# Four weight loads issued by GpSimd instead of SP in a cross-attention and FFN kernel

## The chip, the cores and the metric

The kernel runs on one core of a Trainium2 chip. The core has five engines that follow their own instruction queues: TensorE (PE in the profile: matmuls and transposes), VectorE (DVE), ScalarE (ACT), GpSimd (POOL) and SyncE (SP), which here does nothing but issue DMA transfers. Sixteen DMA engines move the data between HBM and the on-chip memory SBUF. The metric is the device time of one execution in microseconds; lower is better. Before the change it is 720.79 us, the median of 3 runs (720.69 to 720.82).

## The reference

A cross-attention block and a quantized feed-forward block, each on a layer-normed input and each with a residual. x is 8 batches of 112 tokens of width 512; the context is 8 batches of 375 rows of width 256; there are 16 heads of width 128, and the hidden width of the feed-forward block is 2048.

```
x = x + xattn(layernorm(x), ctx, Wq, Wk, Wv, Wo, gq, gk)
x = x + ffn(layernorm(x), W1, B1, W2, B2)

xattn: q = rmsnorm(h @ Wq) * gq;  k = rmsnorm(ctx @ Wk) * gk;  v = ctx @ Wv   (per head)
       out = softmax(q k^T / sqrt(128)) v;  return out @ Wo
ffn:   rows of X and all of W are rounded to int8 steps by their largest absolute value
       gelu(Xq @ W1q^T * scales + B1), quantized again, @ W2q^T * scales + B2
```

Wq is 512 x 2048, Wk and Wv are 256 x 2048, Wo is 2048 x 512, all in float32.

## The kernel before

**Tiling.** The heads are taken in groups of four (NG = 4 groups, 512 columns each), the batches in pairs (NPAIR = 4 pairs). A step on a pair and a group is numbered G = 0 to 15, a step on a batch and a group u = 0 to 31. The weights do not stay on chip: for each G the kernel loads again the column group of Wq (1 MB), Wk (0.5 MB) and Wv (0.5 MB), and the row group of Wo (1 MB). Every row that a load moves is 2 KB long in HBM.

**Work of one G.** Queries (line 532) and keys (650) are made by TensorE; VectorE and ScalarE norm them. Keys, queries and probabilities have to be transposed. Most of that goes by way of HBM: VectorE transposes blocks of 32 x 32, SP sends the blocks to a scratch buffer in HBM (keys: line 707, tile kd; probabilities: 807, pd; queries: 587, qd), and SP fetches them back in the new order (keys: 714, tile kT; probabilities: 817, pT; queries: 619, qr). Then come scores (758), the softmax (771 to 791), the weighted context (860, which reads pT), values (887, which read wv) and the projection (910, which reads wo).

**The quantized weights of the feed-forward block** are made in the first 200 us from eight pieces of 1 MB that SP loads at line 307: VectorE finds the largest value of each piece (line 315) and of all (321), GpSimd takes the largest over the partitions (322), and VectorE scales (328) and rounds.

**Order.** All steps have short names, and four long scripts (line 1214 on) give the order in which the whole kernel is written down: for instance `lq.3` is load_wq(3), `lk`, `lv` and `lo` are the other three loads, `Q0` and `Q1` the queries, `k0` to `k2` the keys, `kf` and `pf` the fetches of kT and pT. In later scripts the numbers are relative to the pair. The function in_written_order (line 77) ties each instruction to the one before it on the same engine, for the engines in this list:

```
ORDERED = (ENG.PE, ENG.DVE, ENG.Activation, ENG.SP)          # line 26
```

GpSimd is not in the list; there the framework (Tile) places instructions by its own rule, and each engine then executes its queue in order. Semaphore waits are put in by Tile for all engines.

**The queue before.** SP issues every transfer. GpSimd issues none: it clears small constants and the four probability buffers at the start (line 111), and does two all-reduces over partitions (line 322, steps ja.0 and ja.1).

**Buffers of the weights.** The tags in wpool decide what a load waits for. wq and wo have one buffer each, wv one, wk two. wq_1 sits in wo's buffer (line 211), wv_15 in one of wk's (226), wo_15 in wq's (232). So a load waits until the last matmul that reads the tile before it in the tag is done: load_wq(G) for the queries of G - 1 (wq_2 for those of G = 0), load_wk(G) for the keys of G - 2, load_wv(G) for the values and load_wo(G) for the projection of G - 1. wq_0, wq_1, wk_1 and wv_0 go to buffers that nothing has used. wk_0 is loaded in two halves with the first context by load_half (line 220), beside the function that the change edits for the others.

**The start.** The first script begins

```
cz.0 lk.0 cz.1 lf.0 lf.1 lx.0 l7.0 gl.0 lc.1 kh.0 jl.0 lk.1 lq.0 jl.3 jl.6 kh.1 xs.1 xs.0 ...
```

lf.0 and lf.1 load the halves of wk_0 and of the first context, lx.0 the first two batches of x, l7.0 the last batch of x, gl.0 the gains, lc.1 the second context (tile cT_1), jl.n the pieces of the feed-forward weights; kh, xs and what follows is work on other engines.

Of the kernel before, what the change touches and what calls it, by code (L numbers as in the profile page):

```python
# [30 lines left out]
def xattn_ffn_kernel(  # L31
# [16 lines left out]
    nc = tc.nc  # L48
    P = 128
# [7 lines left out]
    NG = INNER // (HG * D)  # L57
    GW = HG * D
# [65 lines left out]
    n = 1  # L124
# [84 lines left out]

    def load_wq(G):  # L210
        t = wpool.tile([P, KC, GW], F32, tag="wo" if G == 1 else "wq", name=f"wq_{G}")
        nc.sync.dma_start(out=t, in_=wq[:, bass.ts(G % NG, GW)].rearrange("(k p) n -> p k n", p=P))
        T["wq", G] = t

    def load_wk(G):
        t = T["wk", G] = wpool.tile([P, KCC, GW], F32, tag="wk", name=f"wk_{G}", bufs=2)
        if G > 0:
            nc.sync.dma_start(out=t, in_=wk[:, bass.ts(G % NG, GW)].rearrange("(k p) n -> p k n", p=P))

    def load_half(k):  # L220

# [3 lines left out]
    def load_wv(G):  # L225
        tag, bufs = ("wk", 2) if G == NGG - 1 else ("wv", 1)
        t = wpool.tile([P, KCC, GW], F32, tag=tag, name=f"wv_{G}", bufs=bufs)
        nc.sync.dma_start(out=t, in_=wv[:, bass.ts(G % NG, GW)].rearrange("(k p) n -> p k n", p=P))
        T["wv", G] = t

    def load_wo(G):
        t = wpool.tile([P, HG, C], F32, tag="wq" if G == NGG - 1 else "wo", name=f"wo_{G}")
        nc.sync.dma_start(out=t, in_=wo[bass.ts(G % NG, GW), :].rearrange("(h p) c -> p h c", p=P))
        T["wo", G] = t

    def pad_context(b):
# [26 lines left out]
    def load_biases(_):  # L263
        after(("jr", 2 * NP - 1))
        nc.sync.dma_start(out=b1_sb, in_=b1.partition_broadcast(P))
        nc.sync.dma_start(out=b2_sb, in_=b2.partition_broadcast(P))

    step("lq", NG, load_wq)
    step("lk", NG, load_wk)
    step("lv", NG, load_wv)  # L270
    step("lo", NG, load_wo)
    step("cz", BP, pad_context)
    step("lc", BP, load_context)
# [1128 lines left out]
```

## Time and profile before

| what | value |
|---|---|
| median of 3 runs | 720.79 us (720.69 to 720.82) |
| the profiled execution: its own time | 720.28 us |
| its span, first to last instruction | 718.5 us |
| TensorE clock granted | 0.999 of full speed |
| DMA: all on SP's queue, q1 | 131200 packets, 187.32 MB, 85.1% of 16 engines' span |
| DMA: two queues that fetch instructions | 46 packets, 0.53 MB |
| HBM read, written | 124.55 MB, 59.45 MB |

The profile shows one execution. Busy time is the time in which an engine ran an instruction; the busy time of TensorE's matmuls (PE) and of its weight loads (PEld) overlap. A row "A <- B: 4.7, 3, 2.8" in a table of waits says that A stood idle for 4.7 us in total, 3 times, at most 2.8 us, until B was done. A row of DMA issues gives the tile written, the tensor read, the queue, how many, KB of each and the median time from issue to landing, which is when the data is there. A row of a timeline gives start, duration, engine, line and operation, and in brackets the idle time before it and what ended it.

### The profile page before, as it was taken

The page shows a single profiled execution, that of the slowest core. Times are in us where ns is not written, and L with a number is a line of the kernel's source. Part 1 is how long each engine was busy: PE and PEld are TensorE (multiplying, and loading weights), DVE is VectorE, ACT ScalarE, POOL GpSimd, SP SyncE. Part 2 cuts the span into 40 slices and gives each one's busy share as a digit, 9 for nine tenths or more (in the row PEclk, how much of TensorE's full clock was granted, in tenths as well). Part 3 has the DMA queues.
Part 4 walks back from the last instruction along what each step waited for, and adds up shares of the span by engine and source line. Part 5 has one row for each costly group of instructions (what it writes and reads, how often), then busy time and mean ns, then how long its engine had stood idle before and what let it go on. Part 6 is the DMA issues. An engine that isn't in the chain of part 4 may idle for free.

```text
span 718.5 us, 8555 instructions
## 1 busy us (share of the span) xinstructions
PE 702.7 (98%) x2398; PEld 413.3 (58%) x2410; DVE 537.3 (75%) x1234; ACT 433.6 (60%) x1129; POOL 2.4 (0%) x10
## 2 busy tenths in 40 slices
PE   9999999999999999999999999999999999999976
PEld 4444456655657564745656465564657455667742
DVE  6997888887876677747857787868774898964395
ACT  5677576636475756556466556666755566627325
POOL 0000000000000000000000000000000000000000
PEclk9999999999999999999999999999999999999999
DMA  8799999989988999999898989999999889998201
GB/s 304 266 280 298 294 298 282 301 268 290 282 308 244 293 285 313 269 275 310 227 289 286 295 265 287 287 240 305 292 257 291 237 256 272 259 290 282 34 1 44
DMA packets 131246, 187.85 MB, mean 261 GB/s; under 512 B 34864, under 2 KB 90800, under 8 KB 130560
## 3 DMA queue, kind: packets, MB, share of 16 engines
q1 hardware_dynamic: 131200, 187.32, 85.1%
q8 instruction: 19, 0.31, 0.2%
q14 instruction: 27, 0.22, 0.1%
HBM read 124.55 MB, written 59.45 MB: 256 GB/s over the span
## 4 chain that ended last, share of the span: by engine, by line
PE 85%; DVE 5%; ACT 4%; DMA 3%; SPq 1%; issue 1%; POOL 0%; ACTq 0%; DVEq 0%; POOLq 0%
PE pkk L650 19%; PE pu L860 17%; PE pw L910 13%; PE pq L532 12%; PE sc L758 10%; PE po L887 6%; PE py L1159 2%; PE ph L1080 2%; DMA pT<-pd 1%; PE pkk L660 1%; DMA kT<-kd 1%; ACT probs L780 1%; DMA qr<-q 1%; DMA qss<-s 1%; ACT qsq L547 1%
## 5 line engine op out<-in xcount | busy, mean ns | idle before, releaser
L650 PE MATMUL pkk<-wk,cT 128*128 128x512 f32 x372 | 171.8, 593 | 0.3 <-DVE hid L1089 0.3
L860 PE MATMUL pu<-pT,c 128*128 128x448 f32 (+1 forms) x384 | 152.3, 540 | 1.0 <-DMA pT<-pd 1.0
L860 PEld LDWEIGHTS pu<-pT,c 128*128 128x128 f32 (+1 forms) x384 | 72.5, 190 | 71.3 <-issue 61.7
L780 ACT ACTIVATE probs<-sc,bias,rq 112x375 f32<-112x375 f32 x128 | 84.1, 663 | 47.8 <-DVE bias L773 47.8
L650 PEld LDWEIGHTS pkk<-wk,cT 128*128 128x128 f32 x372 | 70.0, 190 | 72.3 <-issue 60.9
L910 PEld LDWEIGHTS pw<-oT,wo 128*128 128x128 f32 x544 | 98.2, 190 | 9.8 <-issue 6.5
L910 PE MATMUL pw<-oT,wo 128*128 128x224 f32 (+1 forms) x544 | 101.8, 343 | 0.6 <-ACT oT L897 0.6
L532 PE MATMUL pq<-wq,xnT 128*128 128x512 f32 x224 | 100.2, 592 | 0.0
L758 PE MATMUL sc<-kT,qT 128*112 128x384 f32 x256 | 92.4, 486 | 0.3 <-DMA kT<-kd 0.2
L670 ACT COPY kk<-pkk 128x512 f32<-128x512 f32 x96 | 55.2, 580 | 58.6 <-DVE kz L698 25.6
L797 DVE STREAM_TRANSPOSE pz<-probs 128x384 f32<-128x384 f32 x120 | 63.7, 558 | 21.1 <-ACT probs L791 18.2
L791 ACT ACTIVATE probs<-probs,inv 112x375 f32<-112x375 f32 x128 | 72.1, 605 | 8.9 <-DVE inv L788 8.9
L771 DVE TENSOR_REDUCE top<-sc 112x1 f32<-112x375 f32 x128 | 63.8, 535 | 18.0 <-PE sc L758 17.5
L681 DVE TENSOR_REDUCE kss<-ksq 128x4 f32<-128x512 f32 x96 | 63.1, 668 | 14.0 <-ACT ksq L675 14.0
L532 PEld LDWEIGHTS pq<-wq,xnT 128*128 128x128 f32 x224 | 42.4, 190 | 49.6 <-issue 46.5
L758 PEld LDWEIGHTS sc<-kT,qT 128*112 128x112 f32 x256 | 44.7, 177 | 38.9 <-issue 16.7
L675 ACT ACTIVATE ksq<-kk 128x512 f32<-128x512 f32 x96 | 59.5, 628 | 6.4 <-DVE kss L681 6.0
L688 DVE TENSOR_TENSOR kk<-kk,rk 128x512 f32<-128x512 f32 x96 | 62.9, 675 | 0.5
L698 DVE STREAM_TRANSPOSE kz<-kk 128x512 f32<-128x512 f32 x93 | 62.3, 690 | 0.9 <-issue 0.4
L871 ACT COPY wc<-pu 128x448 f32<-128x448 f32 x64 | 33.5, 531 | 36.6 <-PE pu L860 36.6
L887 PEld LDWEIGHTS po<-wc,wv 128*128 128x128 f32 x272 | 49.1, 190 | 8.0 <-issue 4.1
L887 PE MATMUL po<-wc,wv 128*128 128x224 f32 (+1 forms) x272 | 53.1, 344 | 0.0
(122 smaller groups left out, 590.8 us busy)
## 6 DMA issues: line engine op xcount, KB each, us to landing
kd<-kz SPq DMA_DIRECT2D x124, 192.0 KB, 4.0
kT<-kd SPq DMA_DIRECT2D x31, 768.0 KB, 6.4
pT<-pd SPq DMA_DIRECT2D x30, 672.0 KB, 6.1
pd<-pz SPq DMA_DIRECT2D x90, 192.0 KB, 4.4
wq<-in_wq SPq DMA_DIRECT2D x16, 1024.0 KB, 7.7
wo<-in_wo SPq DMA_DIRECT2D x16, 1024.0 KB, 7.8
wv<-in_wv SPq DMA_DIRECT2D x16, 512.0 KB, 5.8
wk<-in_wk SPq DMA_DIRECT2D x15, 512.0 KB, 6.2
```

Source lines behind the costliest of these rows:

```text
L532: nc.tensor.matmul(pq[:, :GW], T["xnT", p][:, k, i * P : (i + 1) * P], T["wq", G][:, k, :], start=(k == 0), stop=(k == KC - 1),)
L650: nc.tensor.matmul(pk[:, :GW], T["cT", batch_of(u)][:, k, j * P : (j + 1) * P], T["wk", u // BP][:, k, :], start=(k == 0), stop=(k == KCC ...
L681: nc.vector.tensor_reduce(T["kss", u][:, j, :], T.pop(("ksq", u, j)).rearrange("p (h d) -> p h d", d=D), AX.X, ALU.add)
L688: nc.vector.tensor_tensor(kv, kv, T["rk", u][:, j, :].unsqueeze(2).to_broadcast([P, HG, D]), ALU.mult)
L758: nc.tensor.matmul(sc[:S, :SKP].rearrange("p (j i r) -> p j i r", j=NJ, r=BK), T["qT", G, i][:, h, :], T["kT", u][:, :, :, h, :].rearrange ...
L771: nc.vector.tensor_reduce(top[:, h : h + 1], T["sc", u, h0 + h][:S, :SK], AX.X, ALU.max, negate=True)
L780: nc.scalar.activation(p_bufs[h][:S, :SK], T["sc", u, h][:S, :SK], AF.Exp, bias=T["bias", u, h0][:, h - h0 : h - h0 + 1], scale=rq_of(u, h ...
L791: nc.scalar.mul(p_bufs[h][:S, :SK], p_bufs[h][:S, :SK], T["inv", u][:, h : h + 1])
L797: nc.vector.transpose(T["pz", u][:, :, :, :, h, :].rearrange("p a f j q -> p j a f q"), p_bufs[h].rearrange("p (j a r) -> p j a r", j=NJ, ...
L860: nc.tensor.matmul(pu[:, : HG * S], T["c", b][: ROWS[j], j, k * P : (k + 1) * P], T["pT", u][: ROWS[j], :, j, :, :].rearrange("p f h q -> ...
L887: nc.tensor.matmul(po[:, (h - h0) * n : (h - h0 + 1) * n], T["wv", G][:, k, h * D : (h + 1) * D], T["wc", G][:, k, h, :, :].rearrange("p b ...
L910: nc.tensor.matmul(pw[:, (c - c0) * n : (c - c0 + 1) * n], T["wo", G][:, h, c * P : (c + 1) * P], T["oT", G][:, h, lo : lo + n], start=(h ...
```

## The change

The four functions that load the column groups of Wq, Wk and Wv and the row groups of Wo call `nc.gpsimd.dma_start` where they called `nc.sync.dma_start`. Sizes, buffers, sources and the scripts are the same. The halves of wk_0, the context, x, the biases, the pieces of the feed-forward weights and all transposes by way of HBM stay with SP. 63 transfers move: 16 each of wq, wv and wo and 15 of wk.

```
     def load_wq(G):
         t = wpool.tile([P, KC, GW], F32, tag="wo" if G == 1 else "wq", name=f"wq_{G}")
-        nc.sync.dma_start(out=t, in_=wq[:, bass.ts(G % NG, GW)].rearrange("(k p) n -> p k n", p=P))
+        nc.gpsimd.dma_start(out=t, in_=wq[:, bass.ts(G % NG, GW)].rearrange("(k p) n -> p k n", p=P))
         T["wq", G] = t
 
     def load_wk(G):
         t = T["wk", G] = wpool.tile([P, KCC, GW], F32, tag="wk", name=f"wk_{G}", bufs=2)
         if G > 0:
-            nc.sync.dma_start(out=t, in_=wk[:, bass.ts(G % NG, GW)].rearrange("(k p) n -> p k n", p=P))
+            nc.gpsimd.dma_start(out=t, in_=wk[:, bass.ts(G % NG, GW)].rearrange("(k p) n -> p k n", p=P))
...
-        nc.sync.dma_start(out=t, in_=wv[:, bass.ts(G % NG, GW)].rearrange("(k p) n -> p k n", p=P))
+        nc.gpsimd.dma_start(out=t, in_=wv[:, bass.ts(G % NG, GW)].rearrange("(k p) n -> p k n", p=P))
         T["wv", G] = t
...
-        nc.sync.dma_start(out=t, in_=wo[bass.ts(G % NG, GW), :].rearrange("(h p) c -> p h c", p=P))
+        nc.gpsimd.dma_start(out=t, in_=wo[bass.ts(G % NG, GW), :].rearrange("(h p) c -> p h c", p=P))
         T["wo", G] = t
```

More of the change, by code (lines that the diff above doesn't have):

```diff
@@ L211, in load_wq @@
         t = wpool.tile([P, KC, GW], F32, tag="wo" if G == 1 else "wq", name=f"wq_{G}")
-        nc.sync.dma_start(out=t, in_=wq[:, bass.ts(G % NG, GW)].rearrange("(k p) n -> p k n", p=P))
+        nc.gpsimd.dma_start(out=t, in_=wq[:, bass.ts(G % NG, GW)].rearrange("(k p) n -> p k n", p=P))
         T["wq", G] = t
@@ L217, in load_wk @@
         if G > 0:
-            nc.sync.dma_start(out=t, in_=wk[:, bass.ts(G % NG, GW)].rearrange("(k p) n -> p k n", p=P))
+            nc.gpsimd.dma_start(out=t, in_=wk[:, bass.ts(G % NG, GW)].rearrange("(k p) n -> p k n", p=P))
     def load_half(k):
@@ L227, in load_wv @@
         t = wpool.tile([P, KCC, GW], F32, tag=tag, name=f"wv_{G}", bufs=bufs)
-        nc.sync.dma_start(out=t, in_=wv[:, bass.ts(G % NG, GW)].rearrange("(k p) n -> p k n", p=P))
+        nc.gpsimd.dma_start(out=t, in_=wv[:, bass.ts(G % NG, GW)].rearrange("(k p) n -> p k n", p=P))
         T["wv", G] = t
@@ L232, in load_wo @@
         t = wpool.tile([P, HG, C], F32, tag="wq" if G == NGG - 1 else "wo", name=f"wo_{G}")
-        nc.sync.dma_start(out=t, in_=wo[bass.ts(G % NG, GW), :].rearrange("(h p) c -> p h c", p=P))
+        nc.gpsimd.dma_start(out=t, in_=wo[bass.ts(G % NG, GW), :].rearrange("(h p) c -> p h c", p=P))
         T["wo", G] = t
```

## The prediction

> **What bounds the kernel now.** I read the busy table first, then TensorE's waits, the busy time by stretch, the DMA issues, SP's own waits, GpSimd's timeline.
>
> ```profile
> span 718.5 us, 8555 instructions
> PE 702.7 (98%) x2398; PEld 413.3 (58%) x2410; DVE 537.3 (75%) x1234; ACT 433.6 (60%) x1129; POOL 2.4 (0%) x10
> ```
>
> ```profile
> 0.00:680.00 680.00, 675.57 (x2232) 398.01 (x2242) 508.37 (x1165) 418.54 (x1101) 2.37 (x10) 1.00 0.90 275
> ```
>
> TensorE is the bound: 98% of the span, and 675.57 of the first 680 us, at granted clock 1.00 (the last three columns are clock, DMA share and GB/s). Its matmuls also start back to back at their shortest spacing (four key matmuls in 1.72 us, 0.43 each, from the first stretch to the last), so the busy time hides no waiting. Of the 4.43 us it is idle before 680 us, 1.19 is the program's start; **3.24 us is all that faster loads could win**. After 680 us no weight is loaded any more (last issue 657.35 us).
>
> The DMA engines are the second limit: 0.91 to 0.94 busy in every stretch from 50 to 600 us. What TensorE still waits for there is two fetches:
>
> ```profile
> PE pu L860 <- DMA pT<-pd: 1.0, 1, 1.0
> ...
> PE sc L758 <- DMA kT<-kd: 0.2, 1, 0.2
> ```
>
> Neither is a weight. The loads that move, and the fetches beside them:
>
> ```profile
> kT<-kd SPq DMA_DIRECT2D x31, 768.0 KB, 6.4
> pT<-pd SPq DMA_DIRECT2D x30, 672.0 KB, 6.1
> ...
> wq<-in_wq SPq DMA_DIRECT2D x16, 1024.0 KB, 7.7
> wo<-in_wo SPq DMA_DIRECT2D x16, 1024.0 KB, 7.8
> wv<-in_wv SPq DMA_DIRECT2D x16, 512.0 KB, 5.8
> wk<-in_wk SPq DMA_DIRECT2D x15, 512.0 KB, 6.2
> ```
>
> 63 transfers, 47.6 MB, a quarter of the 187.85 MB moved; the last column is the median time from issue to landing. From the timelines of SP and TensorE I took for each load its issue, its landing and the first matmul that reads it: the median load lands 6.6 us early, ten less than 3 us early, none late. The same for the 61 fetches of kT and pT: nine land less than 1 us before their first matmul, thirteen less than 1.5 us.
>
> **What goes from SP.** 63 issues; by tile their median durations are 607, 442, 430 and 453 ns (wq, wv, wo, wk), 16 x 0.607 + 16 x 0.442 + 16 x 0.430 + 15 x 0.453 = 30.5 us of SP's time. SP also held other transfers until a weight had landed:
>
> ```profile
> SPq L707 <- DMA wo<-in_wo: 4.7, 3, 2.8
> ...
> SPq L807 <- DMA wq<-in_wq: 3.3, 2, 2.3
> ```
>
> Line 707 sends keys and needs no weight. All such rows together (lines 414, 587, 591, 707, 714, 807, 817, 984, 991 waiting for wq, wo, wv or wk) are 24.9 us, and SP's own waits for TensorE at lines 212 and 228 are 6.2 us. All of it goes. It is worth at most the 3.24 us of TensorE's idle time, at least nothing; I take half, **-1.6 us**, since nearest to it are the two fetch waits (1.2 us).
>
> **What comes to GpSimd.** Its queue is empty but for this:
>
> ```profile
> 0.72 1.48 POOL L111 MEMSET probs<- 128x384 f32 x4 [0.29 <-POOLq L1390]
> 83.58 0.35 POOL L322 PARTITION_ALL_REDUCE absw<-pm_w  x1 [81.38 <-DVE pm_w L321]
> 177.18 0.35 POOL L322 PARTITION_ALL_REDUCE absw<-pm_w  x1 [93.25 <-DVE pm_w L321]
> ```
>
> No row shows GpSimd issuing a DMA. Bounds for one issue: SP's 0.4 us below; above, the 12.3 us of the narrowest window below. I take a few us, nearer SP's rows, and it is hidden: each load now waits only for its buffer and for the loads ahead of it on GpSimd. Following line 209 to 234's tags, the buffer is free after the last matmul of the load before it in the tag; from then to first use there are 12.3 us for wq_9, 13.5 for wq_6, 15.3 for wq_3 and over 17 for the rest, against landings of 5.7 to 11.6 us for wq. So **late weights cost 0** here; without that cover, at 16 us per landing, (16 - 12.3) + (16 - 13.5) + (16 - 15.3) = 6.9 us.
> What queues behind a waiting load on GpSimd: other loads, and the two all-reduces, which VectorE's scaling at line 328 waits for. In script order the first stands behind wq_3, whose buffer is free at 79.3 us, the second behind wq_5 (168.2 us); both are before the all-reduces' inputs (83.58, 177.18). Cost 0, at worst an issue's length of VectorE. Line 26 leaves GpSimd out of the written order, so Tile may turn loads round there; a later load passing a blocked one costs nothing.
>
> **The moved traffic.** GpSimd would issue the median load 15.7 us earlier than SP does. Bytes are the same; what they collide with is not.
>
> *At the start.* wk_1, wq_0, wq_1 and wv_0 have fresh buffers: 3 MB set free when the memsets end at 2.20 us (SP issued them at 5.79, 6.60, 19.66, 36.12). Beside them run x (issued 2.60, landed 8.10) and cT_1 (4.63, landed 10.43).
>
> ```profile
> 8.17 0.69 DVE L171 BATCH_NORM_STATS2 bn<-x 112x6 f32<-112x512 f32 x1 [3.73 <-DMA x<-in_x]
> ```
>
> VectorE stood 3.73 us for x, and has only 0.66 us idle from there to 22 us; keys(1) on TensorE at 11.76 us needs cT_1, 1.33 us after it landed. By 8.10 us 1.37 MB had come, by 10.43 us 1.98 MB: 263 GB/s, begun at about 2.9 us, 2.2 us after SP's first issue. With the same 2.2 us GpSimd's traffic begins at 4.4. Lower bound: it comes too late to touch anything, 0. Upper (estimate from these rows): from 4.4 us SP's transfers run at half rate; cT_1's remaining 1.59 MB take 12.1 us, landing at 16.5, 6.1 us later, less 1.33 cover = 4.8 us on TensorE. (x: 3.8 later, less 0.66.) Middle: 3.05 - 1.33 = **+1.7 us**. What is late next is VectorE's chain to line 688, where TensorE already waits 0.45 us.
>
> *In the middle.* A 1 MB load is 1.05 MB / 285 GB/s = 3.7 us of all engines. A fetch beside a moved load is 0 to 3.7 us later (or as much earlier where the load stood ahead of it). Which fetches are hit is dealt anew. Of the thirteen with under 1.5 us in hand I let a quarter be hit (the weights' share of bytes), by 1.85 us less 0.7 in hand: 13 x 0.25 x 1.15 = **+3.7 us**, and take the 48 others as covered. Ends: 0, and 13 x (3.7 - 0.7) = 39 us if every one were hit.
>
> Sum: -1.6 + 1.7 + 3.7 = +3.8 us. The profiled execution took 720.28 us around its span of 718.5, 0.51 below the median 720.79; on the median the sum gives **724.6 us**.
>
> **Rules of the skill.** The Trainium skill's "DMA: Bandwidth & Descriptors", section "Issuing engines are not separate DMA queues", says that issuing from several engines saves only sequencer time and all of it shares the same 16 DMA engines; the rows here put sequencer time at 30.5 us off the bounding engine, and by that rule alone the sum would be about 0 to -1.6 us.
> "SBUF — State Buffer", section "SBUF: two separate sides", speaks against the change: GpSimd writes the descriptors of its DMAs itself and is locked out while VectorE copies or scales fp32 in SBUF in a two-port mode, with a 620 ns DMA stretched to 3100 ns. VectorE's TENSOR_SCALAR rows here are at most 1.29 us each and some 65 us in all, so by that rule a load would be a few us later, inside its window.
>
> **The rivals.**
> *Same (0.25).* GpSimd's start is slow enough to miss x and cT_1, and the relief of SP balances the collisions: 720.8. For it: only 3.24 us are there to win, 48 of 61 fetches have slack.
> *Faster (0.10).* With no weight ahead of them in SP's queue, kT and pT land sooner; its place is 490 to 600 us, where most of the idle time lies, and it decides once it wins 1.44 us net. All 3.24 us less 1.2 at the start (x 1.9 us late, half its bound, less 0.66): 720.79 - 2.0 = 718.8. For it: the 24.9 us that sends were held. Against: no wait of TensorE is for a weight, and it needs a mild start.
> *Slower by GpSimd's issue (0.20).* A load issued there takes so long that it lands more than 12.3 us after its buffer is free; from that point wq_9 stalls TensorE, then wq_6 and wq_3. At 16 us it is 6.9 us on top of 3.8: 731.5. At 20 us ten loads are late by 31.7 us in sum, 755. Against: 0.4 us on SP.
> *It doesn't do what it says.* If GpSimd's order made loads wait as long as SP did, the start would be unhurt and the time that of "same"; it is in that chance.
>
> **Numbers.** Forecast 0.45, its own range 722.3 to 728. From the cases: faster by over 0.2% (below 719.35; 0.2% is about what a measurement of this kernel can tell from no change) 0.10, within 0.2% 0.25, slower 0.65. The range 719.2 to 733 leaves out most of "faster" and the far part of the late loads.
>
> **What would show it.** In the profile after: the weights' rows issued by POOL; first issues near 2.2 us; x and cT_1 landing after 8.1 and 10.4 us and an idle spot of TensorE between 11 and 20 us; rows of SP waiting for weights gone; TensorE's waits on kT and pT together 2 to 6 us, and none on wq, wk, wv or wo. A wait on a weight would make me wrong on GpSimd's cost; VectorE rows longer than before, on the lock; an unchanged start, on the burst.

## The result, and the profile after

The changed kernel takes **763.1 us** (median of 6 runs, 758.7 to 770.3), the kernel before 720.8 in the same session: a ratio of 1.058 with a 95% interval of 1.0536 to 1.0627, so 42 us slower. Medians are of all runs, ratios of the means of the undisturbed ones, so the two can differ a little. The profiled execution took 760.4 us; all readings of the changed kernel below are from it.

The first rows of its page, then its busy time by stretch (columns: length; busy PE, PEld, DVE, ACT, POOL with the count of instructions; granted clock; DMA share; GB/s):

```profile
span 758.6 us, 8626 instructions
PE 711.1 (94%) x2410; PEld 415.0 (55%) x2410; DVE 538.8 (71%) x1234; ACT 433.6 (57%) x1129; POOL 52.4 (7%) x73
```

```profile
0.00:30.00 30.00, 20.02 (x59) 10.65 (x60) 13.73 (x53) 10.52 (x25) 5.38 (x13) 0.89 0.80 276
30.00:240.00 210.00, 208.28 (x646) 118.11 (x645) 171.84 (x378) 138.16 (x393) 15.57 (x21) 1.00 0.86 275
240.00:300.00 60.00, 54.70 (x165) 30.28 (x164) 37.44 (x85) 30.61 (x90) 5.44 (x6) 1.00 0.91 298
300.00:530.00 230.00, 226.96 (x739) 130.94 (x738) 169.35 (x393) 143.08 (x364) 14.73 (x20) 1.00 0.87 270
530.00:580.00 50.00, 39.77 (x135) 24.02 (x134) 24.85 (x53) 19.26 (x50) 3.62 (x4) 0.93 0.98 215
580.00:640.00 60.00, 58.34 (x194) 34.75 (x194) 47.81 (x117) 38.00 (x92) 3.65 (x5) 1.00 0.87 257
640.00:700.00 60.00, 55.12 (x206) 35.91 (x205) 36.51 (x79) 30.84 (x74) 3.97 (x4) 0.97 0.82 241
```

TensorE's idle time (span less busy time) is 47.5 us; it was 15.8. That is 31.7 of the 40.1 us by which the span grew. The other 8.4 us are in the busy time itself, 711.1 against 702.7 (a part of them only because the trace of the kernel before lacks 12 matmul records of lines 1080 and 1159). The mean granted clock is 0.986 of full speed where it was 0.999; 1.3% of 711 us would be 9 us, and the clock is below 1.00 only in stretches that have idle spots. VectorE's busy time is the old one (537.3). The idle time sits in spots: 10 us in the first 30, 5.3 in 240 to 300, 10.2 in 530 to 580, 4.9 in 640 to 700. Laid over the kernel before, matmul by matmul, TensorE is 10.2 us late by the end of the start, 16.5 after the spot near 285 us (times of the kernel before), 20.1 at 500, 31.8 at 540 and 40 at the end.

What TensorE waits for, in total, times and longest:

```profile
PE pkk L650 <- DMA cT<-in_ctxT: 8.8, 1, 8.8
PE py L1159 <- DMA hqT<-hq: 7.5, 1, 7.5
PE sc L758 <- DMA kT<-kd: 7.4, 7, 2.7
PE pu L860 <- DMA pT<-pd: 4.6, 2, 3.0
```

None of these is a moved load. The second is a transfer that the prediction never named: the transpose of the quantized hidden layer (tile hq) of one batch, which SP issues at line 1073 as one DMA transpose, a transfer that turns the tile on its way. There are five of hq in the kernel, and five of a smaller tile, xq. The two fetches cost 12.0 us where they had cost 1.2. SP's own waits show what is behind them:

```profile
SPq L817 <- DMA pd<-pz: 24.6, 22, 4.3
...
SPq L714 <- DMA kd<-kz: 14.0, 8, 4.6
```

Line 817 fetches pT and has to wait until the stores pd, which it reads back, have landed. In the kernel before, the same two rows were

```profile
SPq L817 <- DMA pd<-pz: 10.3, 14, 1.9
...
SPq L714 <- DMA kd<-kz: 5.1, 7, 1.2
```

SP's rows that wait for wq, wk, wv or wo are gone. From the DMA issues (KB each, median us from issue to landing):

```profile
kT<-kd SPq DMA_DIRECT2D x31, 768.0 KB, 6.6
pT<-pd SPq DMA_DIRECT2D x30, 672.0 KB, 6.9
...
wq<-in_wq POOLq DMA_DIRECT2D x16, 1024.0 KB, 8.4
wo<-in_wo POOLq DMA_DIRECT2D x16, 1024.0 KB, 8.4
wv<-in_wv POOLq DMA_DIRECT2D x16, 512.0 KB, 6.9
wk<-in_wk POOLq DMA_DIRECT2D x15, 512.0 KB, 7.5
```

**The start**, in timeline rows of GpSimd, VectorE and TensorE (start, duration, engine, line, operation; in brackets the idle time before and what ended it):

```profile
2.15 0.84 POOL L218 DMA_DIRECT2D wk<-in_wk  x1
2.99 1.52 POOL L212 DMA_DIRECT2D wq<-in_wq  x2
4.50 0.70 POOL L228 DMA_DIRECT2D wv<-in_wv  x1
```

```profile
12.48 0.69 DVE L171 BATCH_NORM_STATS2 bn<-x 112x6 f32<-112x512 f32 x1 [7.91 <-DMA x<-in_x]
```

```profile
20.30 5.21 PE L650 MATMUL pkk<-wk,cT 128*128 128x512 f32 x8 [8.78 <-DMA cT<-in_ctxT]
```

By 5.2 us GpSimd has issued 3 MB. x lands 9.9 us after its issue (5.5 before), cT_1 15.3 us after (5.8), and TensorE stands still for 8.78 us. The eight matmuls that come next take 5.21 us where they had taken 3.60:

```profile
11.76 3.60 PE L650 MATMUL pkk<-wk,cT 128*128 128x512 f32 x8
```

That is 1.6 us more, and the granted clock was 0.70 in this stretch, from 20.3 to 25.5 us.

The packet records of the trace show how the DMA engines divided their work. From 6 to 18 us they moved 788 packets of GpSimd's queue and 835 of SP's, nearly one for one; but GpSimd's are mostly of 4 KB and SP's of 2 KB at most, so GpSimd got 3.00 MB through and SP 0.95. From 12 to 16 us, 260 of SP's 329 packets were of 4 bytes, most of them rows of the gains gq and gk. These stand ahead of cT_1 in SP's queue and landed 12.5 and 13.6 us after their issue, where it had been 5.3 and 5.4.

**Near 540 us** (520 us in the kernel before): SP's row, the same row in the kernel before, GpSimd's rows, and stretches of 6 us (columns as above):

```profile
537.42 9.73 SPq L1073 DMA_TRANSPOSE hqT<-hq  x1
```

in the kernel before

```profile
517.99 5.46 SPq L1073 DMA_TRANSPOSE hqT<-hq  x1
```

```profile
537.89 0.78 POOL L212 DMA_DIRECT2D wq<-in_wq  x1 [2.03 <-PE pq L532]
547.60 0.75 POOL L233 DMA_DIRECT2D wo<-in_wo  x1 [8.93 <-PE pw L910]
```

```profile
549.00:555.00 6.00, 2.92 (x8) 1.14 (x6) 5.19 (x12) 3.50 (x10) 0.00 (x0) 1.00 1.28 73
555.00:561.00 6.00, 1.56 (x4) 0.58 (x5) 0.27 (x1) 2.73 (x6) 0.00 (x0) 0.57 1.15 183
```

wq_14 goes out 0.47 us after SP has begun the transpose. The transpose holds SP for 9.73 us (5.46 before) and lands after 22.0 us (7.5); wq_14 takes 16.7, the four stores qd behind them 12.3 to 14.3. In the first of the two stretches the DMA engines are counted as more than fully busy (1.28) and move 73 GB/s.

### The profile page after: what moved, and what is told of

Same layout as the page of the kernel before. It is cut to its first block, busy times and chain, and to the rows that moved or that the text cites. A ratio compares the mean times of both kernels' runs of the same rounds, so it can differ in the third digit from the quotient of the medians.

```text
span 758.6 us, 8626 instructions
## 1 busy us (share of the span) xinstructions
PE 711.1 (94%) x2410; PEld 415.0 (55%) x2410; DVE 538.8 (71%) x1234; ACT 433.6 (57%) x1129; POOL 52.4 (7%) x73
## 4 chain that ended last, share of the span: by engine, by line
PE 66%; DMA 16%; DVE 8%; ACT 4%; SPq 4%; issue 1%; DVEq 0%; ACTq 0%
PE pkk L650 17%; PE pu L860 14%; PE pq L532 10%; PE sc L758 9%; PE pw L910 8%; PE po L887 6%; DMA kT<-kd 5%; DMA pT<-pd 3%; DMA cT<-in_ctxT 2%; DMA qr<-qd 2%; DMA qd<-qz 2%; PE ph L1080 2%; PE py L1159 1%; DMA pd<-pz 1%; SPq L807 1%
## 5 line engine op out<-in xcount | busy, mean ns | idle before, releaser
L860 PE MATMUL pu<-pT,c 128*128 128x448 f32 (+1 forms) x384 | 154.2, 545 | 9.2 <-DMA pT<-pd 4.6
L791 ACT ACTIVATE probs<-probs,inv 112x375 f32<-112x375 f32 x128 | 72.1, 605 | 11.5 <-DVE inv L788 11.5
L681 DVE TENSOR_REDUCE kss<-ksq 128x4 f32<-128x512 f32 x96 | 62.9, 667 | 18.7 <-ACT ksq L675 18.6
L675 ACT ACTIVATE ksq<-kk 128x512 f32<-128x512 f32 x96 | 59.5, 628 | 10.3 <-DVE kss L681 10.0
```

Source lines behind the costliest of these rows:

```text
L681: nc.vector.tensor_reduce(T["kss", u][:, j, :], T.pop(("ksq", u, j)).rearrange("p (h d) -> p h d", d=D), AX.X, ALU.add)
L791: nc.scalar.mul(p_bufs[h][:S, :SK], p_bufs[h][:S, :SK], T["inv", u][:, h : h + 1])
L860: nc.tensor.matmul(pu[:, : HG * S], T["c", b][: ROWS[j], j, k * P : (k + 1) * P], T["pT", u][: ROWS[j], :, j, :, :].rearrange("p f h q -> ...
```

## The experiments

Theory after these views: a load costs by **when** it is issued, for it then runs beside SP's short transfers; there are three places, the start, the transpose, and the stores and fetches in between. Rivals: GpSimd's **queue** costs whenever its loads run, or the loss is one thing spread evenly. In the sessions of these runs the kernel before took 721.4 to 722.7 us at the median; each ratio is to its own session. The edits are cut to the lines that matter ("...") and are against the kernel before. Line numbers in the experiments' rows are shifted by a few lines.

**The four first loads back on SP**, the other 59 on GpSimd (the pair of lines at the end stands for wk, wv and wo too):

```
+    def load_queue(kind, G):
+        return nc.sync if (kind, G) in (("lk", 1), ("lq", 0), ("lq", 1), ("lv", 0)) else nc.gpsimd
...
-        nc.sync.dma_start(out=t, in_=wq[:, bass.ts(G % NG, GW)].rearrange("(k p) n -> p k n", p=P))
+        load_queue("lq", G).dma_start(out=t, in_=wq[:, bass.ts(G % NG, GW)].rearrange("(k p) n -> p k n", p=P))
...
```

> The four loads with fresh buffers (wk_1, wq_0, wq_1, wv_0) are issued by SP again, the other 59 by GpSimd. Theory 'start burst': x and cT_1 land at 8.1 and 10.4 us again, the idle 8.8 us of TensorE goes, and with it some 10 us: 751 to 755 us. Rival 'GpSimd's loads cost the same wherever they are': 59/63 of the loss stays, about 760 us.

Measured 753.7 us, ratio 1.0435 (1.0395 to 1.0475), in the range that the theory had: 9.4 us of the loss are the start's. Here the transpose came off worse still, 28.7 us to its landing, again with wq_14 issued 0.5 us after it; TensorE's waits now begin with it:

```profile
PE py L1162 <- DMA hqT<-hq: 14.2, 1, 14.2
PE sc L761 <- DMA kT<-kd: 6.0, 4, 1.8
```

**Only those four on GpSimd**, 59 on SP:

```
+        return nc.gpsimd if (kind, G) in (("lk", 1), ("lq", 0), ("lq", 1), ("lv", 0)) else nc.sync
```

> Only the four loads with fresh buffers are issued by GpSimd, the other 59 by SP. Theory 'start burst': TensorE idle for 8 to 9 us before keys(1) as in the changed kernel, 729 to 732 us. If the start is harmless: 721 us.

Measured 732.9 us, 1.0158 (1.0107 to 1.0208), a little above the theory's 729 to 732, TensorE's wait for cT_1 8.6 us. The start alone costs 11.5 us, alone and on top of the rest about the same.

**The 59 later loads on GpSimd, at SP's times.** As the first experiment, but each load also waits for the last step of TensorE that had ended when SP issued that load in the kernel before. This step is called the load's gate below, and a load that has one is paced; GATES lists them, for instance the scores s2.0 for load_wk(2):

```
+    GATES = {('lk', 2): ('s2', 0), ('lq', 2): ('s2', 1), ...
+        if (kind, G) in GATES:
+            word = GATES[kind, G]
+            edge = mybir.DependencyInfo(mybir.DependencyClass.Sync, mybir.DependencyReason.DATA)
+            ins = list(block.instructions)[-1]
+            tc.add_manual_dep(ins, marks[word], edge, reason="pace")
```

> As the run with the start on SP, but each of the 59 loads on GpSimd also waits for the last TensorE step that had ended when SP issued that load in the kernel before, so its issue falls within some 3 us of SP's. Theory 'timing' (loads set free 16 us earlier collide with fetches and with the DMA transposes): 721 to 726 us. Rival 'queue' (a load from GpSimd slows SP's traffic at whatever time): within 5 us of the run with the start on SP, about 750 us.

Measured 725.6 us, 1.0031 (1.0003 to 1.0060); single runs lie between 720.3 and 727.2, those of the kernel before in the same session between 720.2 and 726.1. The same loads from the same queue cost some 28 us less once they go out at SP's times: the queue as such is not the price. TensorE's waits on the two fetches:

```profile
PE sc L777 <- DMA kT<-kd: 2.5, 3, 2.0
...
PE pu L879 <- DMA pT<-pd: 0.8, 2, 0.5
```

**All 63 on GpSimd, all paced**: as the last, and wk_1 and wq_0 wait for the landing of x, wq_1 and wv_0 for TensorE's steps.

> All 63 loads are GpSimd's, none is SP's; each also waits for what had ended when SP issued it in the kernel before (wk_1 and wq_0 for the landing of x, the rest for a step on TensorE). Theory (the time of the issue costs, at the start and later; the queue does not): 721 to 727 us, TensorE's wait for cT at the start gone, as in the run that paced the 59 later loads. Rival for the start (GpSimd's loads take more of the DMA engines than SP's, whenever they are issued): the start still costs, 730 us or more.

Measured 725.2 us, 1.0048 (1.0023 to 1.0072); no wait for cT_1 is left. GpSimd's rows:

```profile
8.85 0.84 POOL L234 DMA_DIRECT2D wk<-in_wk  x1 [6.65 <-DMA x<-in_x]
9.70 0.78 POOL L227 DMA_DIRECT2D wq<-in_wq  x1
18.04 0.75 POOL L227 DMA_DIRECT2D wq<-in_wq  x1 [7.57 <-PE pkk L669]
```

So all that the change moves can be moved for some 3 us. What is left of a loss is small but clear of zero by both intervals; none of these kernels is faster than the kernel before.

**The 59 later loads on ScalarE**, at their written places, the four first on SP:

```
+        return nc.sync if (kind, G) in (("lk", 1), ("lq", 0), ("lq", 1), ("lv", 0)) else nc.scalar
```

> The start on SP, the other 59 loads issued by ScalarE at their place in its written order: a second queue, but not GpSimd's, and about SP's times. If any second queue beside SP's hurts: about 750 us. If what hurts is GpSimd's early release or GpSimd itself: 721 to 726 us; 59 issues at 0.45 us are 27 us of ScalarE's time, which is 40% idle.

Both expectations missed: **811.1 us**, 1.1253 (1.1191 to 1.1314). TensorE's waits, then SP's:

```profile
PE sc L761 <- DMA kT<-kd: 36.1, 11, 7.8
PE pu L863 <- DMA pT<-pd: 18.2, 9, 4.9
```

```profile
SPq L710 <- DMA wq<-in_wq: 23.3, 3, 8.9
...
SPq L590 <- DMA wk<-in_wk: 20.7, 4, 8.3
SPq L820 <- DMA wv<-in_wv: 15.9, 2, 9.9
```

Line 710 is the store kd, line 590 a store of queries, line 820 the fetch of pT; none needs a weight. SP's rows of this kind sum to 214 us (25.9 before). In the built program Tile hands the transfers of SP and ScalarE the same eight completion semaphores in turn, GpSimd's eight others; a transfer that is next on a semaphore waits for the one that holds it. In the traces of both kernels, none of the 705 transfers on those eight is issued before the one ahead of it on its semaphore has landed. So SP, in order, stood behind weights that ScalarE issued late. The transfers themselves were not slow (kT landed after 5.9 us at the median, 6.4 before). That this sharing is the whole of the 90 us was not tried separately. It also says where the 25 us of the kernel before came from, and that GpSimd is the one engine here that does free SP of them.

**The loads beside the transpose.** First, in the paced kernel, wv_11, wq_14 and wo_11 let go free (their gates taken out of the list):

> As the run with the 59 paced loads, but wv_11, wq_14 and wo_11, the three beside the transpose of hq near 520 us, go out when their buffers come free. Theory (the transpose is held up by GpSimd loads issued within a few us of it): its landing goes from 8 us to over 15 and the time from 725.6 to 733 to 742 us. Rival (the loss there needs the state that all earlier loads leave behind): 724 to 729 us, landing under 10.

Measured 729.5 us, 1.0083 (1.0059 to 1.0108): a miss for both sides, since wq_14 went out 0.63 us *before* the transpose this time, and the transpose landed after 11.5 us. Second, in the 753.7 us kernel those three and wv_12 paced:

> As the run with the four first loads on SP and the others free on GpSimd (753.7 us), but wv_11, wq_14, wo_11 and wv_12 wait for the steps that stood at SP's issue times. Theory (that event alone is some 12 to 17 us of it): the transpose lands after 8 to 10 us, the time is 737 to 744 us. Rival (the loss is spread and would come back at the next step): 749 to 755 us.

Measured 743.5 us, 1.0298 (1.0255 to 1.0341), the landing 8.1 us: 10 us come back, a little less than the theory's 12 to 17. Third, by itself: the kernel before with **one** load moved, wq_14, gated so that it goes out while SP is at the transpose:

```
+        return nc.gpsimd if (kind, G) == ("lq", 14) else nc.sync
...
+    GATES = {("lq", 14): ("k1", 27)}
```

> The kernel before with one load moved: wq_14 alone is GpSimd's, and waits for the TensorE step (k1 of the 27th piece) that ends at 519.1 us, some 1.5 us after SP began the transpose of hq, which then runs by itself on SP. Theory (a GpSimd load issued while SP is at a transpose holds up both, whatever else is changed): the transpose lands after 15 to 29 us instead of 7.5, the time is 727 to 738 us. Rival (it takes the loads of other buffers too, or an issue within half a microsecond): landing under 13 us, 720 to 725 us.

Measured 728.9 us, 1.0092 (1.0068 to 1.0116): one load of 63 costs 6 us. The time is in the range expected, the landing, 13.7 us, short of it. SP's row, GpSimd's, and the stretch in which TensorE paid (busy 2.57 of 6 us; it waits there for kT, a fetch that SP issues behind the transpose). The bracket in GpSimd's row names a store; the gate is the step of TensorE in the edit:

```profile
519.45 5.78 SPq L1092 DMA_TRANSPOSE hqT<-hq  x1
```

```profile
521.57 0.90 POOL L227 DMA_DIRECT2D wq<-in_wq  x1 [344.56 <-DMA kd<-kz]
```

```profile
536.00:542.00 6.00, 2.57 (x6) 1.03 (x6) 3.19 (x7) 5.01 (x11) 0.00 (x0) 0.90 0.94 244
```

By the traces, the landing of this transpose goes with how long after its start wq_14 (wv_11 in one run) is issued from GpSimd: 0.46 to 0.49 us after, in three kernels, 20.1, 22.0 and 28.7 us; 1.9 to 2.1 us after, in two, 13.4 and 13.7; 0.6 us before, 11.5; no moved load issued while SP is at it or in the 3 us before, in seven, 7.5 to 9.5. That isn't a rule for every transpose. Three of the other four of hq were also met in these kernels by loads that GpSimd issued 1.3 to 2.7 us after their start, and they landed after 9.1 us at most (4.7 to 5.9 in the kernel before). Nor is it GpSimd's alone: in the 811.1 us kernel ScalarE issued wv_11 1.43 us after the start of the one near 520 us, and it landed after 12.4. Why this one suffers most the traces don't show.

**Half as early**: each gate half-way between the time the buffer came free and SP's issue time (some 10 us earlier than SP on the mean).

> As the run with the 59 paced loads, but each gate lies half-way between the time its buffer came free and SP's issue time: the loads go out some 10 us earlier on the mean, where the free ones go out some 20 us earlier. Theory (each us of earliness adds meetings with SP's short transfers): between the two, 732 to 745 us. Rival (only issues at once after the buffer comes free hurt, since then several go out together): 724 to 729 us.

Measured 744.2 us, 1.0288 (1.0260 to 1.0317): as the theory has it, at the upper end. Half the earliness costs some two thirds of the loss (18.6 of 28.1 us), with wv_11 at the transpose among it (landing 13.4 us). That the loss goes by which transfers are met, rather than by the microseconds, this run alone doesn't show.

**Which loads.** In the trace of the changed kernel, loads of wv and wo overlap the 30 groups of four stores pd 15.3 times (sum of the overlapped shares), in the kernel before 5.2 times; the expectation's 19.3 and 7.1 count some groups twice. So only wv and wo paced (31 loads), then only wq and wk (28):

> As the run with the four first loads on SP and 59 free GpSimd loads (753.7 us), but the 31 later loads of wv and wo wait for the steps that stood at SP's issue times; wq and wk stay free but for what is queued behind these. Theory (the loss is the meeting of wv and wo, whose buffers come free just before the stores pd, with pd: 19.3 overlaps in the changed kernel against 7.1 before): most of the loss goes, 724 to 735 us. Rival (any load that goes out early costs the same): 735 to 743 us, half of the loss.

> The other half: the 28 later loads of wq and wk wait for the steps that stood at SP's issue times, wv and wo stay free but for what is queued behind these. Theory (wv and wo meet pd): most of the loss stays, 742 to 752 us. Rival (any early load costs the same): 735 to 743 us.

Measured 742.5 us, 1.0280 (1.0262 to 1.0297), and 746.8 us, 1.0325 (1.0289 to 1.0362). The second is as the theory has it, the first is in the rival's range, and the two intervals overlap; but in the first wq_14, free, met the transpose 0.46 us after its start (landing 20.1 us). So the first again with wq_14 paced too:

> As the run that paces wv and wo (742.5 us), and wq_14, which went out 0.46 us after the transpose of hq had been begun there, waits too. Theory (that meeting, with landings of 20 us, is what kept the run from the 724 to 735 us expected): 731 to 737 us, the transpose landing after 8 to 10 us. Rival (the loss is that of free wq and wk loads in general): 739 to 744 us.

Measured 733.5 us, 1.0155 (1.0123 to 1.0187), the landing 8.2 us: 9.0 us back, and in the range that the theory had. This one can be set against the kernel with wq and wk paced, where the transpose also lands early (9.5 us): with wv and wo left free the loss over the 59 paced loads is some 20 us, with wq and wk left free 8 us, with both (743.5 us, near the transpose paced) 18. So most of it is wv's and wo's, though the parts don't add up. Neither half is pure, as a gated load also holds those behind it on GpSimd.

One view sorts most of these runs. A group of four stores, pd or kd, is "met" where moved weights are in flight for 0.6 of the time from its first issue to its last landing, or more; the next column is SP's wait for pd and kd at the two fetches, from its table of waits, then the transpose's landing:

| kernel | time, us | pd met, of 30 | kd met, of 31 | SP's waits for pd + kd, us | landing near 520, us |
|---|---|---|---|---|---|
| before | 720.8 | 10 | 10 | 10.3 + 5.1 | 7.5 |
| all 63 paced | 725.2 | 13 | 9 | 14.7 + 8.1 | 8.1 |
| 59 paced | 725.6 | 12 | 10 | 14.5 + 5.6 | 8.3 |
| one load | 728.9 | 8 | 9 | 9.3 + 4.0 | 13.7 |
| three free | 729.5 | 10 | 12 | 14.1 + 5.1 | 11.5 |
| only the start on GpSimd | 732.9 | 9 | 10 | 9.7 + 5.1 | 8.0 |
| wv, wo, wq_14 paced | 733.5 | 9 | 11 | 19.3 + 10.4 | 8.2 |
| wv, wo paced | 742.5 | 9 | 12 | 20.2 + 7.1 | 20.1 |
| four near the transpose paced | 743.5 | 21 | 16 | 34.0 + 12.8 | 8.1 |
| half as early | 744.2 | 14 | 17 | 17.7 + 16.9 | 13.4 |
| wq, wk paced | 746.8 | 20 | 14 | 31.4 + 6.7 | 9.5 |
| start on SP | 753.7 | 19 | 14 | 28.5 + 10.3 | 28.7 |
| changed kernel | 763.1 | 21 | 15 | 24.6 + 14.0 | 22.0 |

No kernel below 740 us has over 13 of pd or 12 of kd met, and none a landing over 14 us; above 740 us all have 14 or more of each, but for one, which has the landing of 20.1 us. The view doesn't tell the 733.5 us kernel from the paced ones, and the kernel with ScalarE's loads (811.1 us, 9 and 6 met) is slow by its semaphores. What a meeting goes with can be read in the changed kernel: a store of pd lands after 3.4 us on the mean in a free group and after 5.8 in a met one, a fetch of pT after 5.5 when it is free itself and 7.4 when met.

## Why the prediction was right or wrong

Right was the sign, and that the loss is made of collisions. Wrong was the size: +3.8 us against +42. By its steps:

- **What comes to GpSimd: late weights cost 0.** Right. An issue takes 0.75 to 0.86 us on the mean, twice SP's 0.4; loads land after 7 to 8 us at the median, inside their windows; TensorE waits for no weight. The rival "slower by GpSimd's issue" falls, and so does "doesn't do what it says": the first issue is at 2.15 us, where 2.2 was foreseen, and the loads run early enough to hurt.
- **What goes from SP, -1.6 us.** The waits for weights went, as foreseen; no gain is seen. Even paced, with all 63 loads off SP, the kernel is 3 us slower than before, so the relief bought nothing that could be measured. In the changed kernel waits of SP for its own stores stand where the waits for weights were.
- **At the start, +1.7 us.** Right mechanism and place, wrong size: 9.4 to 11.5 us. The step that failed is "from 4.4 us SP's transfers run at half rate": that was meant as the upper bound and gave cT_1 landing at 16.5 us; it landed at 20.2 (4.8 + 15.3). What SP got was about half of the packets, not half of the bytes: from 6 to 18 us 0.95 MB, 79 GB/s, where the step has 131 (263 / 2), because its packets, those of the gains above all, are smaller than GpSimd's. That is read from one trace; no run changed the size of packets or the place of the gains. I then took half of a bound that was too low, and left out the 1.6 us of slower matmuls after the stop.
- **In the middle, +3.7 us.** The main failure, some 28 us with the transpose below and 18 without it, and two steps of it. "Which fetches are hit is dealt anew", with "a quarter be hit (the weights' share of bytes)", took it for chance. It isn't: GpSimd issues a load when its buffer comes free, so at fixed points of TensorE's order, and for wv and wo these lie where the stores pd go out; met groups of pd rise from 10 of 30 to 21. And only the fetches were counted, not the stores that each fetch must wait for; SP's waits for pd and kd at the two fetches rise from 15.4 to 38.6 us. Of these 18 us (743.5 against 725.6) pacing wv and wo takes away 10 (743.5 against 733.5), pacing wq and wk nothing (746.8). How much of it each single meeting costs TensorE was not taken apart.
- The **transpose** has no term in the sum: about 9 to 10 us (753.7 against 743.5; 742.5 against 733.5), 6 alone. The list of SP's transfers that a load can hold up held x, cT_1, kT and pT, and neither the transpose that line 1073 issues nor the gains.
- **The last 2 to 4 us** (both paced kernels) stay open. SP's waits for pd are 4 us longer there than before; whether from the last differences in time or from the queue wasn't told apart.

From the changed kernel back to the one before, the runs give 9.4 (start) + 10.2 (transpose) + 17.9 (stores and fetches) + 4.2 (rest) = 41.7 us. These are the steps of one chain of runs, so that they add up to the whole proves nothing; what supports them is that the start costs about the same alone (11.5), and the transpose in other company (9.0, and 6 by itself). No run issues the loads early from SP's own queue, so how much a second queue adds to an early issue is not told apart.

Three smaller readings of the prediction were off without bearing on this: the 63 loads are 49.8 MB, not 47.6; SP's rows that wait for weights, at the lines it names, add up to 25.7 us, not 24.9; and the DMA engines are 0.88 to 0.95 busy by stretches of 50 us, not 0.91 to 0.94.

Of "what would show it", every sign for the mechanism came (POOL's rows, 2.2 us, x and cT_1 late, the idle spot, SP's rows gone, no wait on a weight, no VectorE row longer); the one with a size, 2 to 6 us on kT and pT, was 12.0.

The Trainium skill's "DMA: Bandwidth & Descriptors", section "Issuing engines are not separate DMA queues", has all issuers share the same 16 DMA engines, so that a second one saves only sequencer time. This case agrees in that no bandwidth came with GpSimd's queue: the DMA engines were busy for 81.2% of 758.6 us against 85.1% of 718.5, 616 and 611 us. What cost the 42 us is that the loads left the order that SP's one queue had given the transfers. No run here tests the lock-out of GpSimd that "SBUF — State Buffer", section "SBUF: two separate sides", tells of: VectorE's busy time stayed (538.8 us against 537.3), and of GpSimd's 63 issues the longest took 1.71 us.

## What to carry to other kernels

Moving a load to an idle queue removes its sequencer time, but also the order that the old queue gave it; if the DMA engines are 0.9 busy, ask what each load will run beside when it goes out as soon as its buffer is free, and follow the chain store, wait, fetch, not the fetch alone. If a queue is to change, keep the issue times with an explicit dependence and compare: here that brought 42 us down to 3. List every transfer of the old queue, above all rare and odd ones such as a DMA transpose, before the sum is made.

## What the runs showed that I had not expected

- One DMA transpose from SP, beside a 1 MB load that GpSimd issues 0.5 us after it, lands after 20 to 29 us instead of 7.5, the load after 16.7 to 17.8 instead of 8.4; the engines are counted as 1.28 busy at 73 GB/s. A load 0.6 us ahead of it does far less (11.5), and three others of its kind, met 1.3 to 2.7 us after their start, land after 9.1 us at most.
- While both queues had work at the start, the DMA engines took nearly as many packets from one as from the other (835 and 788), whatever their size.
- In and after an idle spot of TensorE the granted clock was 0.83 (10 to 30 us) and 0.57 (555 to 561 us); after the first the next eight matmuls took 1.6 us longer.
- Loads issued by ScalarE land sooner than GpSimd's (wq after 6.7 us, not 8.4), and kT and pT beside them too (5.9 and 5.6, not 6.6 and 6.9), with the DMA engines less busy (77.6% of the span, not 81.2); yet that kernel is the slowest of all, 811 us, through what SP waits for.
